# Two levels of Strassen's scheme in the second projection of a graph attention kernel, with the norms' reciprocal roots by Newton steps on VectorE

## The chip, the cores and the metric

One Trainium2 chip, one of its cores, so there is no other core to compare with. The metric is device time of one execution in microseconds (us), median of the runs. Engines: PE is TensorE, PEld its weight loads, DVE VectorE, ACT ScalarE, POOL GpSimd, SP the engine that issues most DMAs.

## The reference, cut to what matters

```python
h   = relu(layernorm(x))                       # x: (128, 64, 512) float32
Wh  = einsum('bnf,hfo->bhno', h, W_heads)      # projection 1, 4 heads
h1  = elu(softmax(mask(leaky(f1 + f2))) @ Wh)  # attention 1
Wh2 = h1 @ W_out                               # projection 2: (2048 -> 512)
out = elu(attention2(Wh2))
y   = relu(out @ w1 + b1) @ w2 + b2 + out      # feed-forward
x   = x + layernorm(y) * gamma + beta
```

All is float32. The 8192 rows are done in 16 groups of 4 tiles of 128 rows. In a group the kernel runs, in software pipelining, a first part (projection 1 of group g beside attention 2 of g-1) and a second part (projection 2 of g, feed-forward of g-1, attention 1 of g+1, norms and transposes of g+2).

## The kernel before: the parts that the change touches

Every large product already uses one level of Strassen's scheme (Winograd's form, 7 block products for 8). `piece` loads a 128x2x256 piece of the weights through a ring of buffers.

```python
def product_n(ms, blocks):            # one of 7 products: 4 heads x 4 matmuls of 256 columns
    ...
    for k in range(2):
        for j in range(2):
            nc.tensor.matmul(bk[:, j, :], a[:, k, ts(j, P)], w[:, k, :], ...)

def project2(g):
    def post(what, a, b=None, to=None):
        ...                           # block differences on GpSimd, result blocks to wh
    return unit(f"b{g}", product_n(ms, ...), post, (1, 5, 6, 2, 7, 3, 4))

def norm_stats(src, tag, t):          # per tile
    nc.vector.bn_stats(st, src); nc.vector.bn_aggr(mv, st)
    nc.vector.tensor_scalar(ve, mv[:, 1:2], EPS, None, ALU.add)
    nc.gpsimd.tensor_tensor(rstd, ve, mhalf, ALU.pow)

def norm1(t):                         # x has buffers of its own (4, shared with the residual's xr); early in the second part
    ...
    nc.scalar.activation(HN[t], X.pop(t), AF.Relu, bias=nb, scale=rstd)
```

`order` lists which product follows which. In the scheme product 3 accumulates onto product 5's PSUM bank, products 7 and 4 onto that of 6. The instructions of each engine are put in order by a scheduler when the kernel is built, from the order of the program and the dependences. I read the traces as if each engine starts them in that order.

## Time and profile before

| | before |
|---|---|
| median of 3 runs (lowest to highest) | 2364.99 us (2364.75 to 2365.51) |
| mean granted clock of the profiled run | 0.992 |
| one group, start of projection 1 to the next | 143.0 us in each of groups 1 to 13 (136.0 in group 0, 137.0 in group 14) |
| waits of TensorE after the first 60 us | 15 us in 10 |
| half clock after the first 55 us | 14 us |

The last two rows are my own count from the trace, and I use it throughout: a wait is where the starts of two matmul passes lie more than 0.64 us apart, less the 0.216 us of a pass; half clock is the sum of the stretches in which the granted clock was 0.50. The page's busy tenths show the same evenness. Each digit is a fortieth of the span:

```profile
PE   6989999999999999999999999999999999999997
...
PEclk7999999999999999999999999999999999999999
```

### The profile page before, as it was taken

Reading aid. Unit: us, or ns where it says so; the run is one execution under the profiler, and the core shown is the slowest. Engines: PE = TensorE matmul, PEld = TensorE weight load, DVE = VectorE, ACT = ScalarE, POOL = GpSimd, SP = SyncE. Lnnn points to the kernel's source line nnn. Section 1 sums busy time; section 2 is a strip of 40 time slices with the busy share of each in tenths; the row PEclk is TensorE's granted clock in tenths of the full one; section 3 lists DMA queues with packets and bytes.
Section 4 is the critical chain, followed back from the end, with each engine's and each line's share of the span. In section 5 each row is a group of like instructions: output and inputs, shape, how many; then the busy total and the mean of one; then the engine's idle time right before and its main releaser. Section 6 shows DMA issues by size and latency. Waiting matters only on the chain.

```text
span 2360.4 us, 32849 instructions
## 1 busy us (share of the span) xinstructions
PE 2317.9 (98%) x11805; PEld 1934.5 (82%) x11805; DVE 1265.5 (54%) x2210; ACT 911.0 (39%) x1623; POOL 1026.7 (43%) x917
## 2 busy tenths in 40 slices
PE   6989999999999999999999999999999999999997
PEld 4868787888878888787887878888788887878885
DVE  7625474554646556474554745556464563744527
ACT  2524425253352533425244251533525344251513
POOL 5664444416344353443524444253443534533333
PEclk7999999999999999999999999999999999999999
DMA  8545353444535445353444544435354453534443
GB/s 308 184 142 193 125 183 127 164 152 132 182 125 178 134 139 179 126 180 129 154 163 129 182 131 161 153 130 181 127 177 132 138 179 127 182 118 164 157 148 106
DMA packets 257809, 366.89 MB, mean 155 GB/s; under 512 B 22216, under 2 KB 145128, under 8 KB 257648
## 3 DMA queue, kind: packets, MB, share of 16 engines
q1 hardware_dynamic: 251024, 343.82, 43.9%
q0 software_dynamic: 4512, 16.78, 1.9%
q10 hardware_dynamic: 2112, 4.19, 0.5%
q8 instruction: 95, 1.56, 0.3%
q14 instruction: 66, 0.54, 0.1%
HBM read 337.45 MB, written 27.26 MB: 155 GB/s over the span
## 4 chain that ended last, share of the span: by engine, by line
PE 94%; DVE 2%; ACT 1%; POOL 1%; issue 0%; DMA 0%; DVEq 0%
PE g_b L322 33%; PE g_a L307 32%; PE g_c L307 8%; PE g_d L322 8%; PE pz L525 4%; PE pa L673 2%; PE pto L700 1%; PE pzS L525 1%; PE pth L371 1%; PE s1pt L472 1%; PE pf L381 1%; PE s1pe L406 1%; DMA x<-in_x_dram 0%; PE s2pt L667 0%; PE pwa L193 0%
## 5 line engine op out<-in xcount | busy, mean ns | idle before, releaser
L322 PE MATMUL g_b<-w,h 128*128 128x256 f32 x2560 | 598.1, 381 | 0.0
L322 PEld LDWEIGHTS g_b<-w,h 128*128 128x128 f32 x2560 | 480.5, 190 | 72.2 <-issue 10.1
L307 PE MATMUL g_a<-z,w 128*128 128x256 f32 x1520 | 361.0, 380 | 1.2 <-DVE g_a L581 0.7
L307 PE MATMUL g_a<-zs_z,w 128*128 128x256 f32 x1504 | 347.9, 379 | 0.0
L307 PEld LDWEIGHTS g_a<-z,w 128*128 128x128 f32 x1520 | 287.6, 190 | 57.9 <-issue 14.3
L307 PEld LDWEIGHTS g_a<-zs_z,w 128*128 128x128 f32 x1504 | 284.8, 190 | 50.5 <-issue 14.3
L322 PE MATMUL g_b<-w,hS 128*128 128x256 f32 x1024 | 243.5, 382 | 0.0
L585 POOL TENSOR_TENSOR hS<-hS,h 128x512 f32<-128x512 f32 x64 | 83.0, 1297 | 366.8 <-DVE hS L549 366.8
L547 ACT ACTIVATE exc<-g_a 128x512 f32<-128x512 f32 x256 | 152.3, 595 | 199.7 <-DVE g_a L581 119.6
L322 PEld LDWEIGHTS g_b<-w,hS 128*128 128x128 f32 x1024 | 191.4, 191 | 30.9 <-issue 6.7
L549 DVE SCALAR_TENSOR_TENSOR h<-exc,g_a 128x512 f32<-128x512 f32 x192 | 131.6, 686 | 136.3 <-ACT exc L548 136.2
L548 ACT ACTIVATE exc<-exc 128x512 f32<-128x512 f32 x256 | 161.6, 631 | 6.5
L615 POOL TENSOR_TENSOR h<-h,h 128x512 f32<-128x512 f32 x64 | 86.7, 1362 | 138.1 <-PE g_b L322 138.0
L332 POOL TENSOR_TENSOR zs_z<-zS,z 128x512 f32<-128x512 f32 x63 | 89.7, 1424 | 128.3 <-PE g_a L307 123.7
L615 POOL TENSOR_TENSOR h<-hS,h 128x512 f32<-128x512 f32 x64 | 81.1, 1268 | 142.4 <-PE g_b L322 142.4
L474 ACT COPY at<-s1pt 128x512 f32<-128x512 f32 x64 | 34.7, 588 | 279.8 <-PE s1pt L472 279.8
L307 PE MATMUL g_c<-ot,w 128*128 128x256 f32 x512 | 123.9, 385 | 0.8 <-DVE n2ve L347 0.8
L322 PE MATMUL g_d<-w,rt 128*128 128x256 f32 x512 | 121.5, 380 | 1.7 <-DVE o L740 1.0
L307 PE MATMUL g_a<-zS,w 128*128 128x256 f32 x496 | 117.2, 379 | 0.0
L639 DVE SCALAR_TENSOR_TENSOR jf<-wh,ao 128x512 f32<-128x512 f32 x128 | 94.3, 776 | 40.3 <-ACT wh L621 40.1
L333 POOL TENSOR_TENSOR zs_z<-z,zs_z 128x512 f32<-128x512 f32 x63 | 85.4, 1357 | 61.1 <-PE g_a L307 40.7
L307 PEld LDWEIGHTS g_c<-ot,w 128*128 128x128 f32 x512 | 93.9, 190 | 21.8 <-issue 9.3
(159 smaller groups left out, 3535.6 us busy)
## 6 DMA issues: line engine op xcount, KB each, us to landing
w<-tc SPq DMA_DIRECT2D x632, 256.0 KB, 2.6
w<-in_L_gnn_W_heads_dram SPq DMA_DIRECT2D x192, 256.0 KB, 2.7
w<-in_L_gnn_W_out_dram SPq DMA_DIRECT2D x192, 256.0 KB, 2.7
w<-in_L_gnn_w_dram SPq DMA_DIRECT2D x96, 256.0 KB, 2.7
x<-in_x_dram SPq DMA_DIRECT2D x66, 256.0 KB, 3.6
xr<-in_x_dram SPq DMA_DIRECT2D x64, 256.0 KB, 2.8
out_dram<-o SPq DMA_DIRECT2D x64, 256.0 KB, 2.1
tc<-pt POOLq DMA_DIRECT2D x20, 512.0 KB, 5.6
```

Of the source, the lines that this page charges most:

```text
L307: nc.tensor.matmul(bk[:, o, :], w[:, k, ts(o, P)], a[:, k, :], start=start and o == 0 and k == 0, stop=k == 1, skip_group_check=True,)
L322: nc.tensor.matmul(bk[:, j, :], a[:, k, ts(j, P)], w[:, k, :], start=start and k == 0 and j == 0, stop=i == len(ms) - 1 and k == 1, skip_g ...
L332: eng.tensor_tensor(s2, s1, a11, ALU.subtract)
L333: eng.tensor_tensor(s4, a12, s2, ALU.subtract)
L525: nc.tensor.matmul(banks[b][:, c, :].rearrange("p (h n) -> p h n", h=H), src[rows, off + c * P:off + (c + 1) * P], at[rows, b], start=True ...
L547: nc.scalar.activation(ex, src, AF.Relu, scale=-1.0)
L548: nc.scalar.activation(ex, ex, AF.Exp, scale=-1.0)
L549: nc.vector.scalar_tensor_tensor(dst, ex, -1.0, src, ALU.add, ALU.max)
L585: nc.gpsimd.tensor_tensor(dst, dst, H1["22"][:, h], ALU.add)
L615: nc.gpsimd.tensor_tensor(dst[:, h], x0[:, h], x1[:, h], ALU.subtract)
L639: nc.vector.scalar_tensor_tensor(junk, WH2[g][:, j], 1.0, ao[:, c, :], ALU.mult, ALU.mult, accum_out=f[:, c, j:j + 1],)
L673: nc.tensor.matmul(pa, AT2[g][:, j, :], WH2[g][:, j, :], start=True, stop=True)
```

## The change

Its intent: in groups 3 to 15 each of the 7 block products of projection 2 is itself done with 7 products of quarter blocks in place of 8, so TensorE passes 128 columns 392 times instead of 256 columns 224 times. The price is more sums: quarter sums of the activations, inner sums of the results, block sums of the weights once, in groups 1 to 3. To make room, norms are batched (4 tiles, or 2), their reciprocal roots come from Newton steps on VectorE in place of a power operation on GpSimd, and x is loaded into the place of the normalised tile. The core of the diff:

```diff
+    def block_sums(p, i):               # 14 of them, in groups 1 to 3
+        y = big.tile(..., tag=f"ot{i}")
+        nc.gpsimd.dma_start(out=y[:, h]..., in_=out_block(...))
+        nc.gpsimd.tensor_tensor(t[:, 0], y12, y11, ALU.subtract)   # and three more
+        nc.gpsimd.dma_start(out=TQ[p][:, :, heads], in_=t)
...
-    def norm_stats(src, tag, t):
-        nc.gpsimd.tensor_tensor(rstd, ve, mhalf, ALU.pow)
+    def norm_stats(srcs, tag, t, gate=False):
+        nc.vector.tensor_scalar(yi, vi, 1, None, ALU.logical_shift_right)
+        nc.vector.tensor_scalar(yi, yi, -1.0, float(0x5F3759DF), ALU.mult, ALU.add)
+        for _ in range(3):
+            nc.vector.tensor_tensor(u, y, y, ALU.mult)
+            nc.vector.tensor_tensor(u, u, hv, ALU.mult)
+            nc.vector.scalar_tensor_tensor(y, u, 1.5, y, ALU.add, ALU.mult)
...
+        if name == "x":                 # x straight into the place of the normalised tile
+            tl = big.tile([P, F], FP, tag="hn", name=f"hn{t}", bufs=G)
...
+    def project2_deep(g):
+        outer = (1, 2, 5, 6, 3, 7, 4)
+        def quarter_sum(p, j):
+            eng = nc.gpsimd if p in (2, 5, 4) else nc.vector
+            ...
+        def after(p, half):             # copies on ScalarE, additions on VectorE
+            ...
+            elif p == 7:
+                nc.vector.tensor_tensor(home(1, 1), bk, home(1, 1), ALU.add)
+        def inner(r, eng):              # five sums of the 7 inner results, one by one
+            eng.tensor_tensor(m[:, :, 1:6:4], m[:, :, 1:6:4], m[:, :, 0:1].to_broadcast(two), ALU.add)
+            ...
+        def part(p, half, j):           # 8 passes of 128 columns
+            for h in range(H):
+                nc.tensor.matmul(bk[:, place[j][1]], x[:, h], w[:, h], ...)
+            ...
+                        if p == 3:
+                            inner(0, nc.gpsimd)
+                        if p == 4:
+                            inner(1, nc.vector)
```

Not shown: two feed-forward sums and R move from GpSimd to VectorE, some attention copies from VectorE to ScalarE, and the ring shrinks from 11 to 10 buffers. The pool that held x and the residual's tiles xr keeps 2 of its 4 buffers, for xr alone. The first statistics of a batch of x are held behind the latest matmul (`gate`).

## The prediction

> **What bounds the kernel now.** I read the page first for the engine that is never idle, then the chain that ended last, then one group of the steady state in windows, then the chain in order of time for the pace of single matmuls.
>
> ```profile
> PE 2317.9 (98%) x11805; PEld 1934.5 (82%) x11805; DVE 1265.5 (54%) x2210; ACT 911.0 (39%) x1623; POOL 1026.7 (43%) x917
> ...
> PE 94%; DVE 2%; ACT 1%; POOL 1%; issue 0%; DMA 0%; DVEq 0%
> ...
> L322 PE MATMUL g_b<-w,h 128*128 128x256 f32 x2560 | 598.1, 381 | 0.0
> ...
> L322 PE MATMUL g_b<-w,hS 128*128 128x256 f32 x1024 | 243.5, 382 | 0.0
> ```
>
> TensorE is busy 98% of the span and is 94% of the chain that ended last. The second projection (g_b) is 2560 + 1024 = 3584 recorded matmuls: 16 groups x 7 products x 4 heads x 4 block matmuls, and each float32 matmul is recorded as two passes. The means of 381 ns are latencies that overlap, so busy time must not be divided for the pace; the chain in order of time gives it.
>
> ```profile
> 1184.52 0.87 PE s1pt L472 x8
> ...
> 1191.45 15.54 PE g_a L307 x72
> ```
>
> A pass that moves 256 columns costs 15.54 / 72 = 0.216 us; one that moves 128 columns (the transposes) costs 0.87 / 8 = 0.109 us. Now one period of the steady state: its second part (project 2, feed-forward, attention 1), its first part (project 1, attention 2), and the two together.
>
> ```profile
> 1102.00:1191.00 89.00, 89.00 (x492) 73.92 (x492) 48.97 (x80) 26.56 (x48) 48.84 (x44) 1.00 0.47 153
> 1191.00:1245.00 54.00, 54.00 (x246) 45.81 (x245) 29.06 (x55) 30.17 (x53) 11.69 (x9) 1.00 0.45 148
> ...
> 1191.00:1334.00 143.00, 143.00 (x736) 119.77 (x735) 78.02 (x134) 56.72 (x101) 60.59 (x53) 1.00 0.46 150
> ```
>
> The columns are length, busy PE, PEld, DVE, ACT, POOL, then clock, DMA share and GB/s. A group takes 143.0 us, TensorE is busy in all of it at full clock, and DVE has 78, ACT 57, POOL 61 us of work. My count of the passes of a group agrees: two projections 2 x 224 x 0.216 = 96.7, feed-forward 112 x 0.216 = 24.2, attention, transposes and scores about 20, together 141 of 143. About 2 us are left for weight loads that can't be hidden where the array changes its row mode. So nothing off TensorE can give time in the steady state; only fewer or shorter passes can.
>
> **What the Trainium skill says.** "TensorE: Matmul & The Clock Gate", Back-to-back issue gap: warm matmuls follow each other at N/2.4 + 2.5 ns. The trace agrees if each float32 pass counts its columns twice: 512/2.4 + 2.5 = 215.8 against 216, 256/2.4 + 2.5 = 109.2 against 109. The same page, LDWEIGHTS (loading the stationary operand): a load takes its columns / 1.2, so 107 ns for 128. This is decisive, because the change halves what each load is used for. The one place where loads of 128 columns stand with almost no matmul work is at the start, at half clock:
>
> ```profile
> 28.44 6.99 PE L193 MATMUL pwa<-aT,wT 128*128 128x2 f32 x32
> ...
> 28.44:35.43 6.99, 6.99 (x33) 6.90 (x32) 5.27 (x17) 1.17 (x2) 6.94 (x9) 0.50 1.02 360
> ```
>
> 6.99 / 32 = 218 ns a pair at clock 0.50, so 109 at full clock: a float32 load really occupies about 109 ns, although its record says 190. "SBUF — State Buffer", SBUF: two separate sides: a VectorE operation with two SBUF inputs and a GpSimd operation that reads SBUF lock each other out. The trace agrees: sums of SBUF tiles on VectorE average 1652 ns in one group, the same size with one PSUM input 692. "DMA: Bandwidth & Descriptors", Specifications: full rate wants transfers of 512 B or more. The new pieces go down to exactly 512 B; no run here shows that size yet.
>
> ```profile
> L332 DVE TENSOR_TENSOR zs_o<-ot,ot 128x512 f32<-128x512 f32 x16 | 26.4, 1652 | 0.6
> ...
> L724 DVE TENSOR_TENSOR rt<-g_c,t_c 128x512 f32<-128x512 f32 x16 | 11.1, 692 | 14.0 <-PE g_c L307 13.9
> ```
>
> **The change part by part.** TensorE: groups 3 to 15 (13 of 16) take 49 products of a quarter block, 49 x 4 heads x 2 passes = 392 passes of 128 columns, in place of 224 of 256. At 109 ns that is 42.7 us against 224 x 0.216 = 48.4: 5.6 us less per group, 13 x 5.6 = 73 us, all of it on the path that sets the end. Load and matmul are now equally long (109 and 109 ns), so the load is just hidden: this is the largest assumption.
>
> VectorE per deep group: 12 quarter sums of 512 elements at 0.69 to 1.65 us (8 to 20); 6 PSUM adds for 3 (+1.6); Newton steps, three sets of 13 small operations at 0.15 us, the duration of the removed addition of eps, less its 8 (+4.7); R and two feed-forward sums moved from GpSimd (+2.1); five inner sums (+2.7); 8 attention copies moved to ScalarE (-5.5). In all +14 to +26: 78 becomes 92 to 104 us of 138. GpSimd: 9 quarter sums at 1.36 (+12), five inner sums (+5), less the power and scale operations 4 x (0.87 + 0.61 + 0.26) = 7 and R and sums 3.5: 61 becomes 68. ScalarE: five more PSUM copies and 8 attention copies, 57 becomes 64. All stay below three quarters, so their cost lies beside TensorE unless a queue is late at one place.
>
> DMA: 21 more pieces of 256 KB per deep group, 13 x 21 x 0.262 = 72 MB, and the one-time block sums 14 x 1.05 = 15 MB: 367 becomes 454 MB, about 197 GB/s over the span, under the 360 that the start reached at a full DMA share (the window above). A piece now feeds 8 x 0.109 = 0.87 us of TensorE, before 1.73; 10 ring buffers look 8.7 us ahead in place of 19, against a landing of 2.6 to 2.7 us (DMA issues of the page). The x tiles are loaded straight into the place of the normalized tiles, so a load waits for TensorE's attention instead of ScalarE; in the built order it stands about ten pieces later in the queue, where TensorE should have passed.
>
> Block sums run in GpSimd's slack in groups 1 to 3 (12 of 54 us busy in the first part): I charge 3 us. New waits in the deep stage: I charge 0.7 us per group, 9 us in all, since 49 part boundaries with more producers replace 28. Start and tail: plus or minus 2. Sum: 2365 - 73 + 3 + 9 = 2304.
>
> **The rivals.** First, the weight load becomes the bound: if load and matmul of equal length don't overlap fully and a pair takes 120 ns, the stage takes 47.0 and the gain falls to 13 x 1.4 = 18 us, about 2358; at the recorded 190 ns a group would lose 26 us and the kernel end near 2700. Against it: the load's 190 ns never lengthened the 216 pace, the start's pairs show 109, and the transposes run at 109 (their loads are shorter, so they prove less). Second, VectorE or GpSimd is late with the quarter sums: each product needs three, in a chain of two, and GpSimd also has 4 block differences (5.4 us) to finish before a later product. If TensorE waits 2 us at three of the seven products, 6 us per group eat the whole gain: about 2370. Against it: these sums are issued a whole product (about 12 us of the stage) ahead. Third, the short look-ahead: TensorE waits for pieces where the deep parts stand without feed-forward between them, at the end of the stage, where a piece of 0.26 MB per 0.87 us is 300 GB/s, not far from the 360 seen. The ring covers about 9 us; a loss of 1 to 2 us per group, 2315 to 2330. Fourth, the smaller waits of TensorE vanish with the power operation: in the window of a whole group above TensorE has none, so this gives nothing in the steady state.
>
> **Range and chances.** Without any new wait 2292; with 2.5 us per group 2327. The range 2286 to 2335 holds both and half of the third rival's worst. Faster by over 2% means under 2317.7, 47 of the 73 us, or up to 2 us of new waits per group: 0.78. Within 2%: 0.19. Slower needs a load-bound array or a serial chain of sums: 0.03.
>
> **What would show it.** Right: the groups of the second projection show 128x128 passes, 13 x 392 = 5096 of them; eight of them take 0.87 us in the chain in order of time; a steady group takes 137.5 to 139 us with TensorE 100% busy and no group of waits of TensorE above about 10 us in total. Wrong: eight take 0.95 us or more (load-bound); idle time before the deep matmuls with VectorE or GpSimd quarter sums as releaser (second rival), or with a DMA of a piece (third); or the first three groups grow by more than 3 us together. The prediction fails altogether if the pair pace is not 109.

## More of the kernel before

Apart from start and end TensorE never rests and never loses its clock. The list of its waits (engine and line, waited for: sum, times, longest) begins with single waits of the start:

```profile
PE pzS L525 <- DVE z L537: 5.5, 1, 5.5
PE s1pt L472 <- DVE s1A L435: 5.4, 1, 5.4
```

## The result, and the profile after

The changed kernel takes 2565.74 us (2564.20 to 2574.12), the kernel before 2364.99: ratio 1.0858, 95% interval 1.0822 to 1.0894. It is slower by 201 us. (Ratios here are the mean time of one kernel's runs over that of the other's of the same rounds, so not quite the ratio of the medians.) The page after, to be laid beside the lines of the page before:

```profile
PE 2341.6 (91%) x13989; PEld 2021.6 (79%) x13989; DVE 1593.0 (62%) x2933; ACT 984.2 (38%) x1784; POOL 1249.8 (49%) x1062
...
PE   6899989899999999989989998998999989899996
...
PEclk8999999999999999999999999999999999999998
...
PE 56%; DVE 32%; POOL 4%; issue 3%; ACT 3%; DMA 2%; SPq 0%; DVEq 0%; POOLq 0%; ACTq 0%
```

The chain that ended last was 94% TensorE; now VectorE has 32% of it, though VectorE is busy only 62% of the span. The tenths for the clock hide its loss (mean 0.964, before 0.992). The waits of TensorE, before single ones, now recur in every deep group:

```profile
PE pth L454 <- ACT hn L440: 51.3, 16, 5.0
PE g_b L766 <- issue: 36.6, 11, 3.3
PE g_a L365 <- ACT t_a L331: 32.1, 13, 4.8
PE g_d L380 <- DVE o L923: 23.9, 14, 3.2
```

One deep group in windows (first part, second part, both; the columns are those of the prediction's windows):

```profile
670.50:725.30 54.80, 52.93 (x233) 44.50 (x232) 32.42 (x55) 28.24 (x51) 21.38 (x18) 0.97 0.56 169
725.30:824.40 99.10, 90.51 (x673) 81.18 (x672) 64.66 (x125) 34.37 (x64) 53.01 (x42) 0.98 0.61 177
670.50:824.40 153.90, 143.45 (x904) 125.67 (x903) 97.08 (x179) 62.61 (x114) 74.39 (x60) 0.98 0.60 174
```

This group takes 153.9 us where I wanted 137.5 to 139. But look at the amounts: DVE 97, ACT 63, POOL 74, DMA 174 GB/s. They are near what was predicted (92 to 104, 64, 68, 197). The work was counted rightly; that it lies beside TensorE was not so.

And the pace of the passes? In the timeline of TensorE 24 of them stand in one line (start, length with the latency of the last):

```profile
810.15 2.84 PE L766 MATMUL g_b<-wq,hS 128*128 128x128 f32 x24
...
812.83 1.06 PE L766 MATMUL g_b<-wq,q 128*128 128x128 f32 x8
```

2.68 us for 24 is 0.1117. Over the trace, starts of successive quarter passes lie mostly 0.111 to 0.112 us apart (mean 0.1116 of those under 0.15), where transposes have 0.109. TensorE does its part, only a little slower than assumed.

**Where a wait comes from.** First, the transposes of the normalised tiles. Of this timeline (start, length, engine, line, operation) I keep the chain alone:

```profile
749.49 0.33 SPq L100 DMA_DIRECT2D hn<-in_x_dram  x1
...
752.04 1.75 DVE L392 TENSOR_TENSOR zs_o<-ot,zs_o 128x512 f32<-128x512 f32 x1
...
753.72 1.27 DVE L414 BATCH_NORM_STATS2 n1st<-hn 128x6 f32<-128x512 f32 x2
...
756.65 1.05 DVE L421 TENSOR_SCALAR n1v<-n1mv 128x4 f32<-128x4 f32 x1
...
762.44 0.16 DVE L437 SCALAR_TENSOR_TENSOR n1nb<-n1mv,n1y 128x4 f32<-128x4 f32 x1
...
762.63 2.22 ACT L440 ACTIVATE hn<-hn,n1nb,n1y 128x512 f32<-128x512 f32 x3 [3.62 <-DVE n1nb L437]
763.50 0.72 PEld L454 LDWEIGHTS pth<-ident,hn 128*128 128x128 f32 x4 [3.74 <-ACT hn L440]
```

The last tile of x is asked for only at 749.49, when attention has left its place. Then follow the statistics, the Newton chain on four numbers per partition (756.65 to 762.60, 5.95 us, a step every 0.2 us and some of 1.0 to 1.2 where GpSimd's long sums run), the activation, and TensorE comes 3.74 us late. In the kernel before x had its own buffers and all this lay earlier. Which part of the chain decides (the late load, the batch of four, the gate or the steps) these lines don't show; run 2 speaks against the steps.

Second, what the profile calls "issue": product 4 adds onto the bank in which product 7 lies, and may start its second half only when VectorE has taken product 7 out (L744).

```profile
816.17 0.68 DVE L923 TENSOR_TENSOR o<-g_d,o 128x512 f32<-128x512 f32 x1
...
818.43 0.75 DVE L933 SCALAR_TENSOR_TENSOR o<-o,n2mv,gs 128x512 f32<-128x512 f32 x1
819.10 0.68 DVE L744 TENSOR_TENSOR wh<-g_b,wh 128x512 f32<-128x512 f32 x1
...
819.88 1.13 PE L766 MATMUL g_b<-wq,q 128*128 128x128 f32 x8 [3.34 <-issue]
```

Product 7's passes had ended at 813.0. VectorE isn't idle from then on. It works through score products, a feed-forward sum and last norms, for which TensorE isn't waiting, and the addition on which it waits stands behind them. Third, the first head of projection 1 waits for a copy that waits for VectorE's addition L330; a last norm (L934), the inner sums (L752 to L756) and score products (jf) stand in front of it:

```profile
826.23 2.50 POOL L929 TENSOR_TENSOR xr<-xr,bs 128x512 f32<-128x512 f32 x2 [11.30 <-DMA xr<-in_x_dram]
...
827.54 1.74 DVE L934 SCALAR_TENSOR_TENSOR o<-o,n2y,xr 128x512 f32<-128x512 f32 x1 [2.77 <-POOL xr L929]
...
832.44 0.69 DVE L755 TENSOR_TENSOR wh<-wh 128x512 f32<-128x512 f32 x1
...
833.50 1.65 DVE L820 SCALAR_TENSOR_TENSOR jf<-wh,ao 128x512 f32<-128x512 f32 x1
...
835.70 0.69 DVE L330 TENSOR_TENSOR g_a<-g_a,s_a 128x512 f32<-128x512 f32 x1
...
837.06 2.44 PE L365 MATMUL g_a<-zs_z,w 128*128 128x256 f32 x8 [3.86 <-ACT t_a L331]
```

Here VectorE does stand idle first, for 2.77 us, until the residual's tiles have been loaded and summed on GpSimd. Over the run that is 41.6 us in 13 places (before: no such wait; what the last norms waited for was the power operation, 0.8 us). The load was issued only at 823.40, behind the store of the first pair of tiles, and its pool has 2 buffers in place of 4. No run changes this alone. Run 6 keeps it (48.4 us) and yet loses nearly all of the first head's waits, so it takes the inner sums as well.

The fourth (L923, feed-forward) is of the same kind. By my count the four make 39.8, 37.4, 33.8 and 20.4 us of 187 us of waits in all.

VectorE's own work became longer too. A score product takes 776 ns in the mean before and 958 after: 0.68 us in both kernels where no long GpSimd sum runs beside it, 1.20 to 1.21 where one does, and that is so for 22 of 128 before and 68 of 128 after (my count from the traces).

**What a wait costs beyond itself.** "TensorE: Matmul & The Clock Gate", section "What's actually happening" in the Trainium skill, says that the array falls to half its clock after an idle window of about 3.4 us and that the window runs free. This trace agrees in the stretches: nearly all are 3.4 or 6.8 us long, 164 us in all (before 14). Of 24 waits of 0.6 to 2.0 us none was followed by one; of 19 waits of 2.0 to 3.5 us, 9 (five of these last 3.38 to 3.40 us, and two come right behind a longer wait); of 23 longer ones, all. Waits that stand alone, over all 17 traces, say more: 2 of 212 from 1.0 to 2.0 us were followed, 40 of 63 from 2.0 to 3.3 us, 162 of 164 from 3.5 us on. So a wait shorter than the page's window can do it. A stretch at half clock loses half its length (passes of 256 columns follow at 0.427 us there, at 0.216 elsewhere), so (164 - 14) / 2 = 75 us; without the parts of the stretches that are waits themselves (24 us, before 3) it is 65. The prediction has no term for this.

### The profile page after: what moved, and what is told of

The parts are those of the page before. It is cut to its first block, busy times and chain, and to the rows that moved or that the text cites. A ratio compares the mean times of both kernels' runs of the same rounds, so it can differ in the third digit from the quotient of the medians.

```text
span 2564.0 us, 38992 instructions
## 1 busy us (share of the span) xinstructions
PE 2341.6 (91%) x13989; PEld 2021.6 (79%) x13989; DVE 1593.0 (62%) x2933; ACT 984.2 (38%) x1784; POOL 1249.8 (49%) x1062
## 4 chain that ended last, share of the span: by engine, by line
PE 56%; DVE 32%; POOL 4%; issue 3%; ACT 3%; DMA 2%; SPq 0%; DVEq 0%; POOLq 0%; ACTq 0%
PE g_a L365 26%; PE g_b L766 9%; PE g_c L365 5%; PE pz L600 4%; PE g_b L380 3%; DVE o L923 2%; DVE o L934 2%; DVE jf L820 2%; PE pa L855 2%; DMA xr<-in_x_dram 2%; PE pth L454 2%; DVE n2st L414 1%; PE pzS L600 1%; PE g_d L380 1%; DVE o L933 1%
## 5 line engine op out<-in xcount | busy, mean ns | idle before, releaser
L365 PE MATMUL g_a<-zs_z,w 128*128 128x256 f32 x1504 | 361.2, 388 | 32.1 <-ACT t_a L331 32.1
L766 PE MATMUL g_b<-wq,q 128*128 128x128 f32 x2184 | 295.3, 281 | 45.3 <-issue 36.6
L766 PEld LDWEIGHTS g_b<-wq,q 128*128 128x128 f32 x2184 | 271.6, 195 | 67.9 <-issue 50.8
L766 PEld LDWEIGHTS g_b<-wq,h 128*128 128x128 f32 x2080 | 262.0, 195 | 20.4 <-issue 14.2
L766 PE MATMUL g_b<-wq,h 128*128 128x128 f32 x2080 | 276.9, 281 | 0.0
L929 POOL TENSOR_TENSOR xr<-xr,bs 128x512 f32<-128x512 f32 x64 | 83.2, 1310 | 223.7 <-DMA xr<-in_x_dram 209.1
L692 POOL TENSOR_TENSOR hS<-h,h 128x512 f32<-128x512 f32 x64 | 92.2, 1465 | 108.4 <-PE g_b L766 95.9
L820 DVE SCALAR_TENSOR_TENSOR jf<-wh,ao 128x512 f32<-128x512 f32 x128 | 120.0, 958 | 29.8 <-POOL wh L756 29.3
L380 PEld LDWEIGHTS g_d<-w,rt 128*128 128x128 f32 x512 | 94.6, 194 | 42.5 <-DVE o L923 27.5
L624 DVE SCALAR_TENSOR_TENSOR hS<-exc,g_a 128x512 f32<-128x512 f32 x64 | 44.0, 688 | 134.6 <-ACT exc L623 134.6
```

The source lines that it names most:

```text
L365: LAST["pe"] = nc.tensor.matmul(bk[:, o, :], w[:, k, ts(o, P)], a[:, k, :], start=start and o == 0 and k == 0, stop=k == 1, skip_group_che ...
L380: LAST["pe"] = nc.tensor.matmul(bk[:, j, :], a[:, k, ts(j, P)], w[:, k, :], start=start and k == 0 and j == 0, stop=i == len(ms) - 1 and k ...
L624: nc.vector.scalar_tensor_tensor(dst, ex, -1.0, src, ALU.add, ALU.max)
L692: nc.gpsimd.tensor_tensor(dst[:, h], x0[:, h], x1[:, h], ALU.subtract)
L766: LAST["pe"] = nc.tensor.matmul(bk[:, place[j][1]], x[:, h], w[:, h], start=first and h == 0, stop=h == H - 1, skip_group_check=True,)
L820: nc.vector.scalar_tensor_tensor(junk.rearrange("p (c v o) -> p c v o", c=2, v=2), WH2[g][j], 1.0, ao[:, c, :].rearrange("p (c v o) -> p c ...
```

## The experiments

Each edit is to the changed kernel unless said. Ratios are to the kernel before (medians 2363.26 to 2364.40 us in the sets), with 95% intervals.

**1. Without the quarter blocks.**

```diff
-DEEP = 3
+DEEP = 99        # and no block sums
```

> The changed kernel without the quarter blocks: every group takes the second projection of the kernel before, no block sums are made; the Newton steps, the batches of norms, the loads into the normalized tiles and the moved sums stay. If these other parts cause the loss (theory, first half), it stays well above the 2365 of before: 2440 to 2520, with transposes waiting for the norms in every group. If the quarter-block stage causes it (rival), it falls to 2360 to 2385.

Measured 2399.17 us, 1.0148 (1.0133 to 1.0163), within 2% of the kernel before. That lies between the two theories and nearer to the rival: the quarter blocks with their sums, meant to give 73 us, cost 167, and the rest of the change 35. Its own wait list has the late norms at its head, and little else:

```profile
PE pth L454 <- ACT hn L440: 24.6, 16, 4.4
```

**2. Power operation on GpSimd in place of Newton steps**, one per batch.

```diff
-        nc.vector.tensor_scalar(yi, vi, 1, None, ALU.logical_shift_right)   # and the steps
+        nc.gpsimd.tensor_tensor(y, v, mhalf[:, 0:n], ALU.pow)
```

> The changed kernel with one edit: the reciprocal roots come from one power operation on GpSimd per batch instead of 12 small VectorE operations; tiles are still normalized in the same batches. My theory (VectorE's in-order queue is late at four places of each group): the 3.8 us wait of the first transposes for the normalized tiles (40 us over the run) goes, with its half-clock stretch, and the waits behind the feed-forward sums shrink: 2565 falls to 2470 to 2510. Rival (the quarter-block stage itself makes TensorE wait, whatever VectorE does with the norms): under 15 us of change, 2550 or more.

Measured 2541.02, 1.0748 (1.0732 to 1.0764): 25 us faster than the changed kernel, between the two theories. The transposes' wait, which should have gone, is still 50.9 us in 15 places. The Newton steps cost something; they are not the cause, nor what makes the norms late.

**3. Both inner sums on GpSimd.**

```diff
-                            inner(1, nc.vector)
+                            inner(1, nc.gpsimd)
```

> The changed kernel with one edit: the inner sums of both halves run on GpSimd. Theory: the wait inside the first head of projection 1 (34 us in 12 places) shrinks since VectorE's queue is free of these five sums there: 2515 to 2545. Rival (the sums are needed at once by the score products, which stand in VectorE's queue ahead of the urgent sum): the score products wait for GpSimd instead and the wait stays or grows, 2560 or more.

Measured 2605.67, 1.1024 (1.1005 to 1.1042): 40 us slower. The rival holds: the first head's wait for its copy grew from 32.1 to 47.1 us by the profile. GpSimd is no free place; the sums are on a path whichever queue has them.

**4. Two feed-forward sums back on GpSimd.**

```diff
-            nc.vector.tensor_tensor(dst, a, dst, ALU.add)
+            eng = nc.vector if what[0] == "c" else nc.gpsimd
+            eng.tensor_tensor(dst, a, dst, ALU.add)
```

> The changed kernel with one edit: the two feed-forward sums that read SBUF go back to GpSimd. Theory: the 1.7 us wait of the feed-forward for a VectorE sum (20 us in 12 places) goes, and little else, as it is too short to lower the clock: 2535 to 2550. Rival (VectorE's lateness there comes from the norms in front, not from these sums): within 8 us of 2565.

Measured 2578.65, 1.0917 (1.0884 to 1.0951). Slower by 13 us in the medians, though the two intervals still overlap a little, and outside both theories. Nothing was gained; the theory that any work taken off VectorE gives time fell here too.

**5. No quarter sums** (products take plain quarters instead; the result is wrong).

```diff
-            if j in (3, 6, 7):
-                return QS[p, j]
+            # all j take a plain quarter; quarter_sum is not called
```

> The changed kernel without the quarter sums (raw blocks stand in for them, so the result is wrong on purpose): 12 sums fewer on VectorE and 9 on GpSimd per deep group, TensorE's instructions the same. Theory (in the deep groups VectorE has more work in the second stage than fits in front of TensorE's next use): the waits at the sum of product 7, at the feed-forward sum and in the first head shrink, 2440 to 2510. Rival (the order and distances of the quarter products on TensorE cause the waits): 2540 or more.

Measured 2539.82, 1.0742 (1.0726 to 1.0758). The 21 quarter sums, which my second rival had named, are worth 26 us only. The number is the rival's to within 0.2 us; but run 6 leaves the order of the products on TensorE as it is, gains 105 us more, and so rules this rival out as the main cause.

**6. No quarter sums and no inner sums** (wrong): run 5 and

```diff
-                        if p == 3:
-                            inner(0, nc.gpsimd)
-                        if p == 4:
-                            inner(1, nc.vector)
```

> The same without the inner sums too (wrong on purpose): all vector work that the second level of the scheme adds, but for the PSUM sums, is gone. Theory: only the wait of the transposes for the normalized tiles is left, with its half clock: 2370 to 2440. Rival: 2500 or more.

Measured 2435.03, 1.0299 (1.0282 to 1.0316). This is in the expected range. The ten inner sums, with quarter sums already gone, are worth another 105 us (taking them out first was not run). They come last in the group: score products wait for them, and VectorE's additions for the next projection stand behind both.

**7. Early norms as before**, on top of run 6: x in own buffers, each tile by itself with the power operation, early in the second part (wrong).

```diff
+        first[5:5] = norms[:1]
+        first[10:10] = norms[1:]
-                norms + scores + [nothing] * 7,
+                scores + [nothing] * 8,
```

> As the run before, and the norms as in the kernel before: x in buffers of its own, loaded early, each tile normalized early by itself with the power operation (still a wrong result on purpose). Theory: the wait of the transposes goes as well, the quarter products show their own speed, 73 us less than before plus small waits: 2290 to 2330. Rival (the quarter products can't run without waits at all): 2365 or more.

Measured 2373.25, 1.0040 (1.0025 to 1.0055). Lower than run 6 by 62, as a removed wait should be, but not under the kernel before: the expected 2290 to 2330 was missed, and the number is the rival's. Its deep groups take 140.9 us in the mean, its groups 1 and 2, which are not even deep, 159.3 and 154.6.

**8. The correct kernel with early norms and the power operation.** The x buffers need room, so the ring has 8 buffers in place of 10.

```diff
-    ring = ctx.enter_context(tc.tile_pool(name="ring", bufs=10))
+    ring = ctx.enter_context(tc.tile_pool(name="ring", bufs=8))
```

> A correct kernel: the changed one with the norms as in the kernel before (own buffers for x, early, power operation), the room taken from the ring of weight pieces (8 in place of 10), all quarter and inner sums kept. Theory: against the run with the power operation alone (2541) the wait of the transposes (47 us in 11 places and its half clock) goes, the other waits stay: 2450 to 2500. Rival 1 (the transposes' wait is only moved to the next late place): within 15 us of 2541. Rival 2 (8 pieces are too few): waits of the quarter products for the weight pieces' DMA appear.

Measured 2444.95, 1.0343 (1.0327 to 1.0358), just under the expected range: 121 us better than the changed kernel, and the waits for the transposes are gone. Rival 2 did not come: the profile puts no wait of TensorE down to the DMA of a piece. What was left at product 7 could now be seen whole. VectorE is idle there, in front of the last norm's multiplication:

```profile
1077.72 0.71 POOL L417 TENSOR_TENSOR n2y<-n2v,mhalf 128x2 f32<-128x2 f32 x1
```

```profile
1078.46 1.74 DVE L934 SCALAR_TENSOR_TENSOR o<-o,n2y,xr 128x512 f32<-128x512 f32 x1 [3.52 <-POOL n2y L417]
1080.13 0.54 DVE L744 TENSOR_TENSOR wh<-g_b,wh 128x384 f32<-128x384 f32 x1
```

The power operation waits on GpSimd behind five inner sums (1071.95 to 1077.76), VectorE waits 3.52 us for it, and product 7's additions stand behind, although its first half had been done since 1074.14. Newton steps would spare VectorE this wait. So each way of making the root has its own queue to suffer in.

**9. Products 7 and 3 exchanged**, in the changed kernel, so that product 7's addition has more time.

```diff
-        outer = (1, 2, 5, 6, 3, 7, 4)
+        outer = (1, 2, 5, 6, 7, 3, 4)
```

> The changed kernel with products 7 and 3 of the outer level exchanged (1,2,5,6,7,3,4, as the kernel before has them), so that product 3 stands between product 7 and product 4, which shares its PSUM bank. Theory (the third stall of a deep group, 3.3 us of waiting in each of 12 groups, 39 us, is only that VectorE's addition for product 7 has just half a product's time, 2.6 us, before product 4 needs the bank; exchanged it has 8.7 us): this stall goes from every group, with the half-clock stretch of 3.4 us behind it (1.7 us lost): 2500 to 2535 us. Rival (VectorE has a backlog and the wait only moves on to the next place, the first head of projection 1): 2550 us or more, with that stall grown from 34 us.

Measured 2567.41, 1.0859 (1.0843 to 1.0876). The named wait did go (37 us in 11 places, now none) and nothing was won: the first head's waits grew from 34 to 46, those of feed-forward from 20 to 33, others came. My theory of one short deadline fell; the rival's "the wait moves on" is what the count shows.

**10. Block sums held in the first part.**

```diff
-            nc.gpsimd.dma_start(
+            behind_pe(nc.gpsimd.dma_start(
```

> The changed kernel, but the first DMA of each block sum waits for TensorE's latest matmul in program order, so that the block sums of groups 1 to 3 stay in the first part of the group, where GpSimd has slack, and don't move up into the second part of the group before. Theory (groups 1 and 2 took 158 and 154 us in place of 144 because GpSimd stands in its queue waiting for the loads of block sums in the second part[...]): groups 1 and 2 fall to 143 to 147 us, together 20 to 26 us saved, 2538 to 2548 us. Rival (it is the amount of work or the DMA traffic, wherever it lies): 2556 us or more.

Measured 2548.26, 1.0787 (1.0763 to 1.0811). Groups 1 and 2 fell from 158.3 and 154.4 to 145.0 and 144.5 us, as the theory says. Before the edit GpSimd stood in its queue, in the second part, for the load of a block to be summed:

```profile
330.94 1.26 POOL L280 TENSOR_TENSOR ty<-y 128x256 f32<-128x256 f32 x1 [3.86 <-DMA y<-tco]
```

With the edit the whole stretch of group 1 and the start of 2 has two waits of TensorE left:

```profile
PE pth L454 <- ACT hn L440: 1.4, 1, 1.4
PE s1pt L554 <- DVE s1A L521: 0.6, 1, 0.6
```

But group 3 grew from 159.9 to 170.0: the last block sums now stand before a sum that its deep product needs. Hence 17 us in all, though groups 1 and 2 alone gained 23.

**11. Both edits on the kernel of run 8.**

> The correct version with early norms and the power operation (2445 us), with both edits above: products 7 and 3 exchanged and the block sums held in the first part. Theory: its waits of VectorE's addition for product 7 (41 us in 12, with half-clock behind them some 20) and of groups 1 and 2 (15 to 25) go: 2355 to 2385 us, about level with the kernel before. Rival (the waits move on): 2405 us or more.

Measured 2459.78, 1.0402 (1.0384 to 1.0419): slower than run 8 by 15. The rival again. The waits at the place of product 7 fell from 38.5 us in 11 places to 10.3 in 10. What is left there is a wait for a weight piece (9.9 us in 11 by the profile, and as much in run 14): the one at 1084.87 was issued at 1079.65, behind a store that waits for VectorE, and landed at 1084.73. And a new one came:

```profile
PE s1pt L547 <- DVE s1A L514: 48.2, 11, 5.4
```

The attention weights' copy stands on VectorE behind a multiplication that waits for the power operation, which stands on GpSimd behind the inner sums, now later by a product. As in run 10 group 3 pays (165.4 us).

**12. The same with Newton steps for the last norms.**

> The same as the run before it in this set, but the last norms of each group keep their Newton steps on VectorE (those of x use the power operation on GpSimd). Theory (Newton steps cost only VectorE's time, some 2 x 11 more operations of 0.16 us a group, 3.5 us, which has slack once the two late places are mended): within 10 us of that run, either side. Rival (they are a cost of their own wherever they stand): 20 us or more slower than that run.

Measured 2473.11, 1.0461 (1.0445 to 1.0476): 13 us slower than run 11, between the two theories. VectorE's waits for the power operation at the last norms (45.6 us in run 11) are gone, but TensorE's for the attention weights are 60.0 us against 55.1.

**13. Non-urgent work moved to where VectorE has slack**, on run 11: all block sums in groups 1 and 2, the second half of the last norms into the next group's first part, the score products held behind the matmuls beside which they stand in the program.

```diff
-            ) + mix(fin[1:], [nothing] + turns + [nothing] * 2))
+            ) + turns)
+            pend = fin[1:]          # run in the next group's first part
+            if g < NG - 1:
+                behind_pe(jf)       # each score product
```

> The correct version with early norms, products 7 and 3 exchanged and block sums held (2460 us), with three moves and no operation more or less: all block sums in groups 1 and 2; the second half of the last norms moved into the first part of the next group; the score products held behind the matmuls beside which they stand in the program. Theory (place in the queue, not amount of work): the waits for the attention weights (48 us in 11) and the one of 14 us in group 3 go, with half-clock behind them: 2340 to 2390 us. Rival (amount of work): the waits move to the first head of projection 1, 2430 us or more.

Measured 2472.69, 1.0461 (1.0445 to 1.0477). The rival's number, and 13 us slower than run 11. The windows of one group (first part, second part):

```profile
810.10:867.00 56.90, 51.98 (x233) 43.03 (x232) 43.45 (x76) 28.49 (x52) 21.53 (x17) 1.00 0.50 156
867.00:956.60 89.60, 88.24 (x674) 79.54 (x673) 50.62 (x73) 33.52 (x64) 57.99 (x53) 1.00 0.71 205
```

The second part is now clear, with a single wait of 1.5 us, and at full clock. The first part, which takes 51.0 without quarter blocks (run 15), takes 56.9: the moved work has brought its waits along. A group takes 146.5 us. Groups 1 and 2, with all the block sums, take 167.0 and 159.3.

**14. The same with product 3 before 7.**

> As the run before it in this set, but with the outer products in the order of the changed kernel (3 before 7). Theory: with VectorE's queue cleared, the 2.6 us that product 7's addition has are nearly enough: within 15 us of that run. Rival (the order matters once the backlog is gone): slower by 20 us or more, with waits before product 4.

Measured 2479.57, 1.0489 (1.0468 to 1.0509): 7 us slower than run 13, within the expected 15.

**15. Run 8 without quarter blocks** (ring of 10 again), as a base.

> The correct version with early norms and the power operation (2445 us) without quarter blocks and without block sums: nearly the kernel before, with some VectorE and GpSimd sums exchanged. Both theories: 2360 to 2380 us; the stall before the transposes is gone (17.5 us of the 36 in the version without quarter blocks and with late norms, 2399 us). If it stays near 2399, the late norms were not that version's cost.

Measured 2363.45, 1.0001 (0.9984 to 1.0018): level with the kernel before.

```profile
764.70:815.70 51.00, 51.00 (x232) 43.39 (x232) 26.64 (x52) 28.25 (x51) 11.71 (x9) 1.00 0.51 156
815.70:907.10 91.40, 91.40 (x506) 76.65 (x505) 53.08 (x83) 27.93 (x51) 43.50 (x39) 1.00 0.47 148
```

TensorE is busy in all of it. Against run 1 this base has early norms, per tile, with the power operation: together they are worth 36 us. Against run 8 it says what quarter blocks (and 8 ring buffers for 10) cost in the best arrangement that I found: 81 us.

No version beat the kernel before by a margin that the runs can tell.

## Why the prediction was wrong, point by point

**The passes: right in kind, over-sized.** The load does not become the bound, and 13 x 392 = 5096 passes of 128x128 are in the trace. But a pair takes 0.1116 us, not 0.109, so a group saves 48.4 - 43.7 = 4.7 us instead of 5.6. At the switches between kinds of matmul loads show (in the kernel before a switch to or from the 64-row product z takes 0.307 us in place of 0.216), about 0.9 us more per second part (excess of the spacing, 3.9 us besides the one wait in run 13 against 3.0 in run 15). With that wait taken off, the second part of run 13 is 89.6 - 1.5 = 88.1 against 91.4: 3.3 us, or 43 in all, where the sum had 73.

**"Their cost lies beside TensorE unless a queue is late at one place": this is the step that failed.** The amounts were right, and I concluded from busy shares below three quarters (VectorE measured 97 of 153.9, 63%) that the engines have room. The queue was late at four places in every deep group, because VectorE takes its work strictly in order and urgent additions stand behind work that has no deadline, or behind work that itself waits for GpSimd and a load. The term "0.7 us of new waits per deep group" was 11.6 us (mean of groups 3 to 14, none in these groups before); the waits of the whole run grew by 172 (187 - 15).

**The rivals.** The second named the right engine but the wrong work. Quarter sums, issued a product ahead, are worth 26 us (run 5). The inner sums, which I gave 2.7 and 5 us of work and no place, are worth 105 (run 6, with the quarter sums gone), because they stand at the end of a chain: product, inner sum, score product, and next to them the additions of the next projection. The first rival (a load-bound array) and the third (short look-ahead) did not come true in the changed kernel; no DMA of a piece stands among its larger waits (runs 11 and 14 have one). Pieces in 512 B packets landed in 3.5 to 3.7 us, those in 2 KB in 3.5. The fourth, that nothing is gained from the power operation, fits the record. "A serial chain of sums" had been given a chance of 0.03: it was named, and held for unlikely. Two slips in the sums, which decide nothing: "about 2370" leaves out the prediction's own 3 and 9 us, and "without any new wait 2292" leaves out the 3.

**x in the place of the normalised tile, "where TensorE should have passed": wrong.** In the group shown the last load lands at 752.4, 1.3 us before the first statistics, so the norms come just before the transposes. The batch of four and the gate may do their share; no run takes these apart. Late norms, with Newton steps, cost 36 us in the kernel without quarter blocks (run 1 against run 15), and in the changed kernel the waits for the transposes were the largest sum.

**Block sums, 3 us: mis-sized.** Groups 1 and 2 took 158.3 + 154.4 against 2 x 143.0: 27 us. Of this 3 us go to the late norms (both groups take 144.5 in run 1, which has these and no block sums), so 24 to the block sums. They did have the amount of slack on GpSimd that I counted, but the built order had moved their loads into the second part, where an in-order queue that waits for a DMA holds up everything behind it (run 10).

**Half clock: not considered.** 65 us, as worked out above.

Together: -43 for the passes, +172 for waits, +65 for half clock, +4 for the start (projection 1 begins at 58.9 instead of 54.6) make +198, against +201 measured. The 3 us left over are within what these counts can tell.

**What stays open.** Exchanging products or moving work to the part with more slack cleared each named place, and the wait came up at the next one (runs 9, 11, 13). So with this much VectorE and GpSimd work I found no order that fits; that none exists isn't shown. Run 7 gives a measure of what there was to win: even without any quarter or inner sum a deep group takes 140.9 us against 142.3 in run 15, so 1.4 x 13 = 18 us, under 1% of the time. These groups still hold 1.6 us of waits each by my count, so without any wait it would be about 3.0 x 13 = 39 us, near the 43 above. Untested are more buffers for xr, and the load, batch and gate of the early norms one by one.

## What to carry to other kernels

Where TensorE is busy all the time, a change that trades its passes for sums on other engines must be judged by deadlines, not by busy shares: for each new sum ask what stands behind it in the same in-order queue, and how many microseconds TensorE has until it needs that. Count a wait of more than about 2 us as more than itself (40 of 63 lone waits of 2.0 to 3.3 us, 162 of 164 of 3.5 us or more), since TensorE's clock may halve after it, for 3.4 us or more. And when one named wait is removed and the time stays, read the wait list again before removing the next: here the wait had only moved on.

## What the Trainium skill lacked or had wrong

- "TensorE: Matmul & The Clock Gate", "What's actually happening": it gives an idle window of about 3.4 us for the fall to half clock. Over the 17 traces lone waits of 2.0 to 3.3 us already brought it in 40 of 63 cases, and those of 3.5 us or more in 162 of 164; the stretches of 3.4 and 6.8 us agree with it.
- The same page, "Back-to-back issue gap" and "LDWEIGHTS": neither says what a float32 pair costs. The first gives the formula that the prediction used as the gap of an isolated matmul, and about 81 ns at 128 columns and 131 at 512 for a stream of loads and matmuls; here streams of float32 pairs, with columns counted twice, keep to the formula (0.216 us for 256 columns). A pass of 128 columns with a new load of 128 columns each time follows at 0.1116 us, 2% above the 0.109 of transposes and of the estimate from the page.
- No page that I read says how the two ways to a reciprocal root compare inside a full kernel: the chain of Newton steps on four numbers took 5.95 us on VectorE, with steps of 0.16 us, some growing to 1.0 to 1.2 us beside GpSimd's sums, and cost 25 us in all against the power operation (run 2).
